# A graph layer on one core: other row loads, third convolution weights, planner's clock and order of streams

## The chip, the core and the metric

The kernel runs on one core of a Trainium2 chip. Its engines run side by side, each with its own queue of instructions: TensorE (PE, with its weight loads shown as PEld) multiplies matrices, VectorE (DVE) and ScalarE (ACT) work on tiles, GpSimd (POOL) does small operations and issues transfers, SyncE (SP) issues transfers. An engine works its queue in order; where an instruction needs a result of another engine or of a transfer, it waits for a semaphore, and all that is behind it in the queue waits too. The metric is the device time of one execution in microseconds (us); the median of several executions counts. Everything is computed in 32-bit floats.

## The reference, cut to what matters

There are 32 graphs of 512 nodes with 256 features (`x`), and a 0/1 matrix of 512 x 512 for each (`adj`). With `h = relu(layernorm(x))`, the output is `x` plus one graph layer of `h`:

```python
h1 = relu(bn1(conv1d(hT, conv1_w)))            # width 1, over the nodes
x_conv = relu(bn2(conv1d(h1, conv2_w, 8)) + hT)  # 17 taps, padding 8
s = h @ w_se.T + b_se                          # 3 numbers for a node
A = exp(-|s_n - s_m|^2) * adj
x_nmp = A @ relu(h @ w_msg.T + b_msg)
gi = concat(x_conv, x_nmp) @ w_ih.T + b_ih     # 512 -> 768
gh = h @ w_hh.T + b_hh                         # 256 -> 768
r, z = sigmoid(gi_r + gh_r), sigmoid(gi_z + gh_z)
out = x + (1 - z) * tanh(gi_n + r * gh_n) + z * h
```

## The kernel before

**Five streams.** The work is written as five generators (`streams`, from line 1778 on): *rows* makes the input of the long convolution (the width-1 convolution of each graph's turned features, `conv1`, line 528); *begins* turns the normalized features of later graphs, channels on partitions (`begin`, line 1230); *graphs* makes messages, the 512 x 512 kernel matrix, its masking and the gathering (`graph`, line 1282); *conv* is the convolution of 17 taps (`convolution`, line 980); *gates* computes the gates and the output (`gates`, line 1324), with seven products for a block of four times two for all graphs but the first and the last.

**The convolution.** The features of all graphs are cut into units of 18 nodes, and these into seven groups (`STARTS`). The 17 taps are not multiplied one by one: 25 products (numbered `m`, 25 to a group) of transformed inputs (`X2`, made on DVE by `operands`) with transformed weights are summed into the result (`summed`). A product has two weight matrices `w[0]`, `w[1]` of 128 x 2 x 256 and three input phases. In the first group four block products are formed for each `m`. In the later six groups three do: the third uses the sum `w[2] = w[0] + w[1]`, its result is copied to a second bank by ACT (`ps_c`), and the two others use differences of the inputs (`xd`, function `ends`). One product of the 25 (`LONE`, number 6) needs `w[1]` alone.

**Where weights come from.** In the first group `weights_first` (line 723) makes the 25 pairs on DVE and ACT, and `store_w` (line 720) stores each to a DRAM tile `WD[n]`, which has room for three, from POOL's queue. From the second group on `weights_again` (line 765) allocates tiles in a ring of six (`RING`, name `w`) and loads them on SP's queue. In the second group only `w[0]` and `w[1]` are loaded; `third_weight` (line 788) adds them on DVE into the third tile and stores that, from POOL, into `WD[n][:, 2]`. From the third group on all three are loaded. `third_weight` is called from the convolution for the product at hand and the next one, and from the background work (`background`, line 1700).

**Rows and their tiles.** The turned features of a graph are in DRAM (`HD[b]`, written by POOL). `load_row` (line 335) loads them on SP's queue into a tile named `hT`, of which there are two, for a convolution group that needs the graph; `begin` uses the same ring of two tiles for turning new graphs. In `all_rows` (line 1747) the next row's load is put off with `later` until about the time at which the planner's clock has a tile free.

**What sets the order.** All instructions are written in an order worked out while the program is built. A planner keeps a clock for each engine (`now` is that of PE): every operation is given a modelled duration and starts after the modelled ends of what it needs (`after`, line 126; `note`, line 139; `region`, line 102, gives the part of a tile that is touched). Transfers are modelled in `Engine.dma_start` (line 205) with an issue time, a flow rate and eight lanes in flight. A generator yields the time from which it can go on, or a condition. The loop at the end (line 1844 on) takes, among the streams that can go on now (`able`), the one whose own progress clock is least, except at those numbered choices where the table `OTHERS` names the second or third in that order instead. After each step `fill` (line 1722) writes what was put off (`later`), evacuates finished convolution results and, while DVE is free within 1.5 us of the clock, writes background work: norms, inputs and weights of the convolution, its sums, the third weights. The clock only orders instructions; on the chip each engine runs as its semaphores let it.

Of the kernel before, what the change touches and what calls it, by code (L numbers as in the profile page):

```python
# [10 lines left out]
ALU = mybir.AluOpType  # L11
PSUM = bass.MemoryType.PSUM
# [38 lines left out]
def kernel(  # L51
# [50 lines left out]
    def region(a):  # L102
        step = a.ap[0][0]
        size = 1 + sum((c - 1) * s for s, c in a.ap[1:])
        if a.tensor.name in ON_DRAM or step == 0:
            return 0, 1, a.offset, a.offset + size + step * (a.ap[0][1] - 1)
        p, f = divmod(a.offset, step)
        return p, p + a.ap[0][1], f, f + size
# [40 lines left out]
    class Pool:  # L149
        def __init__(self, pool, bufs, on_dram=False):  # L150
            self.pool, self.bufs, self.on_dram, self.rings = pool, bufs, on_dram, {}
            self.made, self.born = [], 0.0

        def tile(self, shape, dtype, **more):
            t = self.pool.tile(shape, dtype, **more)
            self.made.append(t.tensor.name)
            BORN[t.tensor.name] = self.born
            if self.on_dram:
                ON_DRAM.add(t.tensor.name)
            elif "name" in more:  # L160
                ring = self.rings.setdefault(more["name"], [])
                n = more.get("bufs", self.bufs)
                if len(ring) >= n:
                    BORN[t.tensor.name] = released(ring[-n]) + HAND
                ring.append(t.tensor.name)
            return t
# [7 lines left out]

    ON_DRAM = set()

    def pool_of(where, name, bufs, **more):
        pool = where.enter_context(tc.tile_pool(name=name, bufs=bufs, **more))
        return Pool(pool, bufs, more.get("space") == bass.MemoryType.DRAM)

# [19 lines left out]
    class Engine:  # L200
# [4 lines left out]
        def dma_start(self, dst, src, **more):  # L205
            run = 4 * min(dst.ap[-1][1], src.ap[-1][1])
            name = "P" if self.name == "POOL" else "H"
            lanes = LANES.setdefault(name, [0.0] * 8)
            at = max(self.free, after("DMA", [dst], [src]), lanes[0])
            if name == "P":  # L210
                issue = 1.1 if run < 512 else 0.78 if run == 1024 else 0.55
            else:
                issue = 0.53 if run < 512 else 0.43 if run == 1024 else 0.37
            self.free = at + issue
            rate = 150e3 if run < 512 else 330e3
            flow = (self.free + 1.85, 4 * elements(dst) * dst.shape[0] / rate)
            FLOW.append(flow)
            FLOW.sort()
            del FLOW[:-96]
            end = 0.0  # L220
            for arrives, cost in FLOW:
                end = max(end, arrives) + cost
                if (arrives, cost) == flow:
                    break
            lanes.pop(0)
            lanes.append(end)
            note("DMA", [dst], [src], end)
            self.engine.dma_start(dst, src, **more)  # L228
            return end
# [80 lines left out]
    XS, HT, HB, HR, HR_AT, HG, XN, XR = {}, {}, {}, {}, {}, {}, {}, {}  # L310
    NORMS, NORM_AT = {}, {}
    HD = {b: dram.tile([P, ND, N], F32, name=f"hd{b}") for b in range(B)}
# [16 lines left out]
    def load(b, xs=None):  # L329
# [3 lines left out]
        NORM_AT[b] = done(XS[b])  # L333

    def load_row(b):
        if b not in HR:
            settle_stores()
            HR[b] = front.tile([P, ND, N], F32, name="hT", bufs=2)
            sp.dma_start(HR[b], HD[b])
            HR_AT[b] = done(HR[b])  # L340
# [379 lines left out]
    def store_w(dst, src):  # L720
        later(act.free + 0.3, lambda: pool.dma_start(dst, src))

    def weights_first():

# [9 lines left out]
        for j1 in ORDER:  # L734
# [12 lines left out]
            for j2 in ORDER:  # L747
# [7 lines left out]
                for k in range(2):  # L755
                    for i in range(ND):
                        act.activation(
                            w[k][:, i, :], gg[i][:, k, :], AF.Copy, scale=GSCALE[j1] * GSCALE[j2]
                        )
                    store_w(WD[len(WS)][:, k], w[k])  # L760
                WS.append(w)
                W_AT.append(act.free + LAG)
                yield 0.0

    def weights_again():


        for m in range(25, 25 * NG):
            W_BASE.append(taken)
            w = {}  # L770
            for k in (1,) if m % 25 == LONE else (2, 0, 1):
                yield
                w[k] = new_w()
                if k < 2 or m >= 50:
                    sp.dma_start(w[k], WD[m % 25][:, k])
            WS.append(w)
# [4 lines left out]
    def load_weights(done):  # L781

        while len(WS) >= 25 and taken < done + RING and next(again, 0) is None:
            pass

    thirds = set()

    def third_weight(m):
        if m in thirds or m % 25 == LONE:
            return  # L790
        thirds.add(m)
        w = WS[m]
        dve.tensor_tensor(w[2], w[0], w[1], op=ALU.add)
        later(dve.free + 0.4, lambda: pool.dma_start(WD[m % 25][:, 2], w[2]))
        W_AT[m] = dve.free + LAG

# [183 lines left out]
    def convolution():  # L980
# [28 lines left out]
        for g in range(NG):  # L1009
# [9 lines left out]
            for n in range(25):  # L1019
# [8 lines left out]
                yield lambda: len(X2) > m and len(WS) > m  # L1028
                if 25 <= m + 1 < 50 and W_AT[m + 1] <= now:
                    third_weight(m + 1)  # L1030
                for k in (m, m + 1):
# [4 lines left out]
                if exp_waits:  # L1036
                    yield lambda: not exp_waits
                    yield bank_at
                if 25 <= m < 50:
                    third_weight(m)  # L1040
                    yield W_AT[m]
                w, x2 = WS[m], X2[m]
# [187 lines left out]
    def begin(b):  # L1230
# [4 lines left out]
        if b >= TURNED:  # L1235
# [6 lines left out]
            for o in range(ND):  # L1242
                blocks(xb[:, o, :], XD_[b].rearrange("(k i) d -> i k d", i=32), o)
            yield max(done(xb), front.free("hT", 2))
            settle_stores()
            HT[b] = front.tile([P, ND, N], F32, name="hT", bufs=2)
# [13 lines left out]
        yield lambda: b not in NORMS  # L1260
        yield NORM_AT[b]
        turning = True
        for d in range(ND):
# [436 lines left out]
    def background():  # L1700
# [9 lines left out]
        if sum_some():  # L1710
            return True
        for m in range(max(25, at_product), min(len(WS), 50)):
            if m not in thirds and m % 25 != LONE and W_AT[m] <= now:
                third_weight(m)
                return True
        for _ in range(3):
# [4 lines left out]

    def fill():
        while LATER and LATER[0][0] <= now:
# [3 lines left out]
        for b in (gating, gating + 1):  # L1727
            if b in HB:
                load_conv(b)
                if dve.free < now + 1.5:  # L1730
                    residual(b)
                    data_sums(b)
        while dve.free < now + 1.5 and background():
            pass
# [12 lines left out]
    def all_rows():  # L1747
# [5 lines left out]
        for g in range(1, NG):  # L1753
            for b in batches(g):
                yield lambda: (
                    freed >= g - 1 and begun > b and not turning and at_product >= 25 * g - 4
                )
                if b == batches(g)[0]:
                    zeros(g)
                rows_wait = True  # L1760
                yield front.free("hT", 2) - 0.5
                load_row(b)
                if b + 1 in batches(g) and b + 1 < begun:
# [6 lines left out]
    def all_gates():  # L1770
# [19 lines left out]
    OTHERS = {  # L1790
# [15 lines left out]
    }  # L1806
# [37 lines left out]
    while streams:  # L1844
# [11 lines left out]
        choices += len(able) > 1  # L1856
        name = able[min(OTHERS.get(choices, 0), len(able) - 1)] if len(able) > 1 else able[0]
        waits = 0
# [11 lines left out]
        elif got is not None:  # L1870
            clock[name] += (now - began) / streams[name][1]
        fill()

# [48 lines left out]
```

## Time and profile before

| | |
|---|---|
| runs (us) | 1994.66, 1997.48, 1999.35; median 1997.48 |
| the profiled execution | 1992.31 us, span 1990.5 us |
| granted TensorE clock, mean | 0.997 of full speed |
| PE busy | 1959.9 us, 98% of the span, 9691 matmuls |
| DVE / ACT / POOL busy | 1470.5 (74%) / 873.6 (44%) / 483.1 us (24%) |
| transfers | 378.91 MB, 190 GB/s over the span |
| weights: loads on SP / stores on POOL | 414 / 74, 256 KB each |

The span runs from the first to the last instruction of the profiled execution; its own time has a little more around it. Busy times of PE count modelled ends of pipelined matmuls, so "busy" is not yet full speed. A line like `PE ps_g L259 <- DMA hT<-hd: 3.2, 7, 1.0` in the view of waits reads: matmuls of line 259 writing `ps_g` waited for the transfer from `hd` to `hT`, 3.2 us in all, in 7 times, 1.0 us at longest. The lines 241, 259 and 228 are those of helpers through which all operations, matmuls and transfers go, so tiles tell them apart: `ps_c` is the convolution's bank, `ps_g` that of rows, messages and gathers, `ps_acc` that of the gates, `w` and `wd` the convolution's weights on chip and in DRAM, `hd` and `hT` the turned features in DRAM and on chip.

### The profile page before, as it was taken

How to read it: one execution, taken by the hardware profiler on the slowest of the kernel's cores; microseconds unless marked ns; L12 is line 12 of the kernel's file. 1: busy time of each engine (PE TensorE's matmuls, PEld its weight loads, DVE VectorE, ACT ScalarE, POOL GpSimd, SP SyncE). 2: the span in 40 equal slices, each digit the busy share in tenths (PEclk: the TensorE clock that was granted, in tenths of full speed). 3: DMA queues.
4: the chain of work that ended last, by engine and by line, in shares of the span. 5: the costliest groups of instructions: out<-in, count | busy, mean ns of one | idle time of the engine just before them, and what ended most of it. 6: DMA issues, size and time to landing. Idle time of an engine off the chain costs nothing. (4 is left out here: it accounts for less than half of the span.)

```text
span 1990.5 us, 28285 instructions
## 1 busy us (share of the span) xinstructions
PE 1959.9 (98%) x9691; PEld 1441.3 (72%) x9691; DVE 1470.5 (74%) x2559; ACT 873.6 (44%) x1755; POOL 483.1 (24%) x627
## 2 busy tenths in 40 slices
PE   8999999999999999999999999999999999999998
PEld 4877767768676777776777776777776777776774
DVE  6789788969888587875877776868784877765443
ACT  6654653354534455334463335453334453324221
POOL 2222122223112132212232122222221221113232
PEclk9999999999999999999999999999999999999999
DMA  7546878879898789879797888699976877576564
GB/s 272 178 172 216 276 233 206 222 191 240 224 231 215 183 199 207 205 186 224 161 240 172 209 179 230 172 235 202 207 164 179 183 181 157 154 153 125 94 101 35
DMA packets 578176, 378.91 MB, mean 190 GB/s; under 512 B 457664, under 2 KB 475488, under 8 KB 576896
## 3 DMA queue, kind: packets, MB, share of 16 engines
q1 hardware_dynamic: 419760, 279.15, 50.8%
q0 software_dynamic: 157184, 97.81, 26.8%
q8 instruction: 77, 1.26, 0.3%
q14 instruction: 67, 0.55, 0.1%
q10 hardware_dynamic: 1088, 0.13, 0.0%
HBM read 278.94 MB, written 114.56 MB: 198 GB/s over the span
## 5 line engine op out<-in xcount | busy, mean ns | idle before, releaser
L228 POOL DMA_DIRECT2D out_dram<-o_sb x252 | 276.1, 1719 | 583.2 <-DVE o_sb L241 528.6
L259 PEld LDWEIGHTS ps_c<-xd,w 128*128 128x128 f32 x2304 | 285.4, 190 | 44.9 <-ACT ps_c L241 32.2
L259 PEld LDWEIGHTS ps_c<-x,w 128*128 128x128 f32 x2032 | 256.7, 191 | 50.0 <-issue 32.3
L259 PE MATMUL ps_c<-xd,w 128*128 128x135 f32 (+1 forms) x2304 | 290.6, 279 | 1.9 <-ACT ps_c L241 1.4
L259 PE MATMUL ps_c<-x,w 128*128 128x135 f32 (+2 forms) x2032 | 265.6, 279 | 2.9 <-ACT z L241 2.2
L259 PE MATMUL ps_g<-at,msg 128*128 128x512 f32 x512 | 226.4, 593 | 1.5 <-DVE at L241 1.5
L241 DVE TENSOR_TENSOR ps_acc<-ps_acc,r 128x256 f32<-128x256 f32 x120 | 51.5, 429 | 233.8 <-PE ps_acc L259 217.3
L259 PE MATMUL ps_acc<-hTb,whh 128*128 128x512 f32 (+2 forms) x532 | 211.4, 495 | 0.5 <-ACT r L241 0.5
L259 PE MATMUL ps_acc<-xnb,wih 128*128 128x512 f32 (+2 forms) x532 | 209.7, 495 | 2.1 <-DVE ps_acc L241 2.1
L259 PE MATMUL ps_acc<-xconv,wih 128*128 128x512 f32 (+2 forms) x532 | 210.4, 493 | 0.2 <-DVE ps_acc L241 0.2
L259 PEld LDWEIGHTS ps_g<-at,msg 128*128 128x128 f32 x512 | 96.0, 190 | 113.5 <-issue 106.0
L259 PE MATMUL ps_acc<-t,wsum 128*128 128x256 f32 x720 | 175.2, 379 | 0.0
L259 PEld LDWEIGHTS ps_acc<-t,wsum 128*128 128x128 f32 x720 | 134.9, 190 | 33.4 <-issue 16.8
L259 PEld LDWEIGHTS ps_acc<-xconv,wih 128*128 128x128 f32 x532 | 98.6, 190 | 50.4 <-issue 41.4
L259 PE MATMUL ps_g<-wmsg,hTg 128*128 128x259 f32 x496 | 125.5, 383 | 1.9 <-DVE msg L241 1.9
L259 PEld LDWEIGHTS ps_acc<-xnb,wih 128*128 128x128 f32 x532 | 95.7, 190 | 40.7 <-issue 28.1
L259 PE MATMUL ps_acc<-t,wih 128*128 128x256 f32 x480 | 123.2, 379 | 0.0
L259 PEld LDWEIGHTS ps_acc<-hTb,whh 128*128 128x128 f32 x532 | 93.9, 190 | 39.2 <-issue 30.4
L259 PE MATMUL ps_g<-hT,w 128*128 128x512 f32 (+8 forms) x296 | 119.1, 549 | 3.2 <-DMA hT<-hd 3.2
L241 DVE TENSOR_TENSOR x<-x 128x544 f32<-128x544 f32 (+2 forms) x175 | 120.5, 707 | 0.3
L241 ACT ACTIVATE h<-ps_g,bn_shift,bn_scale 128x252 f32<-128x252 f32 (+8 forms) x212 | 87.0, 485 | 56.1 <-PE ps_g L259 55.9
L241 ACT ACTIVATE ps_c<-ps_c 128x270 f32<-128x270 f32 (+1 forms) x144 | 55.9, 388 | 126.2 <-PE ps_c L259 126.1
(156 smaller groups left out, 3202.0 us busy)
## 6 DMA issues: line engine op xcount, KB each, us to landing
w<-wd SPq DMA_DIRECT2D x414, 256.0 KB, 3.9
m_sb<-in_adj_dram SPq DMA_DIRECT2D x384, 64.0 KB, 3.8
wd<-w POOLq DMA_DIRECT2D x74, 256.0 KB, 3.5
hT<-hd SPq DMA_DIRECT2D x33, 512.0 KB, 4.5
hd<-hT POOLq DMA_DIRECT2D x32, 512.0 KB, 6.0
hTb<-hd SPq DMA_DIRECT2D x32, 512.0 KB, 4.8
xnb<-nd SPq DMA_DIRECT2D x64, 256.0 KB, 3.2
out_dram<-o_sb POOLq DMA_DIRECT2D x252, 64.0 KB, 4.8
```

Source lines behind the costliest of these rows:

```text
L228: self.engine.dma_start(dst, src, **more)
L241: getattr(self.engine, op)(*tiles, **more)
L259: nc.tensor.matmul(ps, lhsT, rhs, **more)
```

## The change

Row loads: `row_free` says whether the tile that the next `hT` would take is not one of a row still in use or of a graph being turned (`HTS` lists what took the tiles, None for a graph being turned). `load_row` does nothing while it is false; `all_rows` and `begin` wait for it.

Third weights: `store_sum` stores `w[0]` to `WD[n][:, 2]` and, at the planned end of that, adds `w[1]` to it by an accumulating store, both from POOL's queue, in the first group. In the second group `w[2]` is loaded like the others; `third_weight` is gone.

Clock: transfers are taken to land 1.0 us later, those of POOL another 0.75 us; POOL's issue of small runs is taken as 0.66 us in place of 1.1; a PSUM tile counts as touched as a whole.

Order: a new table `OTHERS`. A pick of 4 or 5 takes the first or second stream and leaves out the background work of the `fill` after it.

```diff
+        if a.tensor.name in ON_PSUM:
+            return 0, P, 0, N
         if a.tensor.name in ON_DRAM or step == 0:
...
             if name == "P":
-                issue = 1.1 if run < 512 else 0.78 if run == 1024 else 0.55
+                issue = 0.66 if run < 512 else 0.78 if run == 1024 else 0.55
...
-            flow = (self.free + 1.85, 4 * elements(dst) * dst.shape[0] / rate)
+            flow = (self.free + (2.6 if name == "P" else 1.85), 4 * elements(dst) * dst.shape[0] / rate)
...
             lanes.append(end)
+            end += 1.0
             note("DMA", [dst], [src], end)
...
+    def row_free():
+        return len(HTS) < 2 or not (HTS[-2] in HR or HTS[-2] is None and turning)
+
+    def row_in(b):
+        load_row(b)
+        return b in HR
+
     def load_row(b):
-        if b not in HR:
+        if b not in HR and row_free():
+            HTS.append(b)
             settle_stores()
...
+    def store_sum(dst, a, b):
+
+        def first():
+            end = pool.dma_start(dst, a)
+            later(end, lambda: pool.dma_start(dst, b, accum_op=ALU.add))
+
+        later(act.free + 0.3, first)
...
                     store_w(WD[len(WS)][:, k], w[k])
+                if len(WS) != LONE:
+                    store_sum(WD[len(WS)][:, 2], *w)
                 WS.append(w)
...
                 w[k] = new_w()
-                if k < 2 or m >= 50:
-                    sp.dma_start(w[k], WD[m % 25][:, k])
+                sp.dma_start(w[k], WD[m % 25][:, k])
...
-    thirds = set()
-
-    def third_weight(m):
-        if m in thirds or m % 25 == LONE:
-            return
-        thirds.add(m)
-        w = WS[m]
-        dve.tensor_tensor(w[2], w[0], w[1], op=ALU.add)
-        later(dve.free + 0.4, lambda: pool.dma_start(WD[m % 25][:, 2], w[2]))
-        W_AT[m] = dve.free + LAG
...
                 yield lambda: len(X2) > m and len(WS) > m
-                if 25 <= m + 1 < 50 and W_AT[m + 1] <= now:
-                    third_weight(m + 1)
...
-                if 25 <= m < 50:
-                    third_weight(m)
-                    yield W_AT[m]
...
             yield max(done(xb), front.free("hT", 2))
+            yield row_free
+            HTS.append(None)
             settle_stores()
...
         yield NORM_AT[b]
+        yield row_free
+        HTS.append(None)
         turning = True
...
-        for m in range(max(25, at_product), min(len(WS), 50)):
-            if m not in thirds and m % 25 != LONE and W_AT[m] <= now:
-                third_weight(m)
-                return True
...
-    def fill():
+    def fill(lean=False):
...
-        while dve.free < now + 1.5 and background():
+        while not lean and dve.free < now + 1.5 and background():
             pass
...
                     freed >= g - 1 and begun > b and not turning and at_product >= 25 * g - 4
+                    and (b in HR or row_free())
                 )
...
                 yield front.free("hT", 2) - 0.5
-                load_row(b)
+                yield lambda: row_in(b)
...
     OTHERS = {
-        8: 1, 11: 1, 41: 1, 43: 1, 57: 1, 70: 1, 73: 2, 84: 2, 95: 1, 102: 1, 104: 1, 110: 1,
...
+        1: 2, 8: 1, 16: 5, 35: 1, 39: 1, 52: 4, 55: 1, 62: 1, 86: 4, 87: 1, 98: 4, 108: 2, 118: 1,
...
-        name = able[min(OTHERS.get(choices, 0), len(able) - 1)] if len(able) > 1 else able[0]
+        pick = OTHERS.get(choices, 0) if len(able) > 1 else 0
+        name = able[min(pick % 4, len(able) - 1)]
...
-        fill()
+        fill(pick > 3)
```

More of the change, by code (lines that the diff above doesn't have):

```diff
@@ L149, with __init__ @@
     class Pool:
-        def __init__(self, pool, bufs, on_dram=False):
-            self.pool, self.bufs, self.on_dram, self.rings = pool, bufs, on_dram, {}
+        def __init__(self, pool, bufs, on_dram=False, on_psum=False):
+            self.pool, self.bufs, self.rings = pool, bufs, {}
+            self.on_dram, self.on_psum = on_dram, on_psum
             self.made, self.born = [], 0.0
@@ L157, in tile @@
             BORN[t.tensor.name] = self.born
+            if self.on_psum:
+                ON_PSUM.add(t.tensor.name)
             if self.on_dram:
@@ L173, in free @@
             return released(ring[-n]) + HAND if len(ring) >= n else 0.0
-    ON_DRAM = set()
+    ON_DRAM, ON_PSUM = set(), set()
     def pool_of(where, name, bufs, **more):
         pool = where.enter_context(tc.tile_pool(name=name, bufs=bufs, **more))
-        return Pool(pool, bufs, more.get("space") == bass.MemoryType.DRAM)
+        return Pool(pool, bufs, more.get("space") == bass.MemoryType.DRAM, more.get("space") == PSUM)
     const = pool_of(ctx, "const", 1)
@@ L310 @@
     XS, HT, HB, HR, HR_AT, HG, XN, XR = {}, {}, {}, {}, {}, {}, {}, {}
-    NORMS, NORM_AT = {}, {}
+    NORMS, NORM_AT, HTS = {}, {}, []
     HD = {b: dram.tile([P, ND, N], F32, name=f"hd{b}") for b in range(B)}
```

32 rows, old and new, of the table OTHERS are left out of this document.

## The prediction

> **What bounds the kernel now.** I read the page first, then the busy times by stage, then who made the tensor engine (PE) wait. The page says that PE is the bound almost everywhere:
>
> ```profile
> span 1990.5 us, 28285 instructions
> PE 1959.9 (98%) x9691; PEld 1441.3 (72%) x9691; DVE 1470.5 (74%) x2559; ACT 873.6 (44%) x1755; POOL 483.1 (24%) x627
> PE   8999999999999999999999999999999999999998
> ```
>
> PE is not busy for 1990.5 - 1959.9 = 30.6 us. The change adds and removes no needed matmul, so it can win only from these 30.6 us, and from matmuls that run slowly. Busy times by stretch of the span (PE, PEld, DVE, ACT, POOL, granted clock, DMA share, GB/s) show where they lie; the cuts are the start, the seven convolution groups as I read them off the trace, and the gates alone at the end:
>
> ```profile
> 0.00:50.00 50.00, 41.82 (x149) 24.41 (x150) 31.84 (x93) 30.39 (x66) 14.46 (x34) 0.93 0.74 271
> 100.00:250.00 150.00, 147.15 (x907) 114.14 (x908) 126.75 (x214) 80.93 (x188) 34.28 (x67) 1.00 0.68 220
> 250.00:512.00 262.00, 259.37 (x1342) 190.02 (x1341) 221.22 (x383) 121.39 (x246) 65.89 (x93) 1.00 0.84 222
> 512.00:760.00 248.00, 244.00 (x1211) 180.30 (x1210) 193.42 (x331) 113.31 (x230) 55.28 (x73) 0.99 0.87 209
> 1010.00:1260.00 250.00, 249.99 (x1211) 184.16 (x1211) 182.80 (x327) 107.68 (x221) 60.51 (x73) 1.00 0.84 199
> 1804.00:1990.00 186.00, 177.41 (x628) 117.20 (x626) 78.75 (x135) 57.02 (x87) 59.03 (x60) 1.00 0.57 91
> ```
>
> The start lacks 50.00 - 41.82 = 8.2 us and the end 186.00 - 177.41 = 8.6 us. At the start PE waits for the first data and norms; at the end the gates are the only stream left, so no order of streams exists there to change. What lies between, 30.6 - 8.2 - 8.6 = 13.8 us, is what an order can win. The stretch 1010 to 1260 shows that this can be nothing at all (249.99 of 250.00). The waits of PE from 50 to 1804 us (total, times, longest) name the causes:
>
> ```profile
> PE ps_g L259 <- DMA hT<-hd: 3.2, 7, 1.0
> PE ps_c L259 <- ACT z L241: 2.9, 3, 2.0
> PE ps_g L259 <- DVE msg L241: 1.9, 1, 1.9
> PE ps_g L259 <- DVE at L241: 1.5, 3, 0.8
> PE ps_c L259 <- ACT ps_c L241: 1.4, 3, 0.5
> PE ps_g L265 <- ACT hT L241: 0.7, 1, 0.7
> PE ps_c L259 <- ACT w L241: 0.6, 1, 0.6
> PE ps_c L259 <- DVE veps L241: 0.4, 1, 0.4
> PE ps_acc L259 <- DVE ps_acc L241: 0.2, 1, 0.2
> ```
>
> They sum to 12.8 us. No single wait owns them: each is a place where the written order sent PE to something that came later on the chip than the planner's clock thought. The longest also cost clock (same columns as the stretches above):
>
> ```profile
> 600.00:603.00 3.00, 0.96 (x3) 0.18 (x2) 2.78 (x4) 2.58 (x6) 0.40 (x2) 0.97 0.63 192
> 603.00:607.00 4.00, 4.00 (x18) 3.68 (x19) 4.00 (x8) 0.43 (x2) 0.58 (x1) 0.60 0.59 186
> ```
>
> After the 2.0 us stall near 600 us, 4.00 us ran at 0.60 of the clock: 4.00 x 0.40 = 1.6 us more. Within reach of the order: 12.8 + 1.6 = 14.4 us.
>
> **The change part by part.**
>
> *Third weights.* Removed: 24 adds on DVE, 24 stores of their result on POOL in the second group. Added: in the first group, after each of 24 weight pairs, one plain store and one accumulating store into the third slice, both on POOL (48 issues); in the second group, 24 loads of 256 KB on SP. The add, and what waited for it:
>
> ```profile
> L241 DVE TENSOR_TENSOR w<-w 128x512 f32<-128x512 f32 x24 | 16.3, 681 | 1.2 <-DMA w<-wd 1.2
> PEld ps_c L259 <- DVE w L241: 1.8, 3, 0.8
> PEld ps_c L259 <- DMA w<-wd: 3.0, 4, 0.8
> ```
>
> DVE gets back 24 x 0.681 = 16.3 us, but it is not the bound: in 250 to 512 us it is busy 221.22 of 262.00. Only the weight loads of PE waited for the add (1.8 us in 3 times), and they overlap matmuls; the matmul waits above have no row for it. The gain lies between 0 and 1.8 us; I take 0.5, since the prefetching weight load had most of it to spare. Against it stands that the third weight now comes by a load, and weight loads waiting for landings cost PEld 3.0 us over the kernel, so the loss is at most as large again. I set the two together at 0.
>
> The stores use the POOL queue and the DMA engines of the first group. POOL row, landing times and the ACT writes of the weights up to 236 us, then the DMA load of 42 to 232 us:
>
> ```profile
> L228 POOL DMA_DIRECT2D wd<-w x50: 539/540/602, 42.6 to 211.8; - x50
> DMA to landing us min/median/max: 2.3/3.4/13.6
> L241 ACT ACTIVATE w<-gg x60: 399/408/438, 41.6 to 211.0; 128x256 f32<-128x256 f32 x60
> 42.00:232.00 190.00, 27.13 (x50) 1.00 0.62 210
> q0 software_dynamic: 6240, 20.98, 28.7%
> ```
>
> POOL: 48 x 0.540 = 25.9 us more in 190 us, where in 100 to 250 us it is busy 34.28 of 150.00. The accumulating store waits for the plain one to land, at the head of POOL's queue if it is issued early; the planner issues it only when its own clock says landed. Behind it on POOL wait stores of normalized rows and messages, and the small powers that finish the norms (ACT's norms wait for those, and the turned rows for ACT). With the median of 3.4 us hardly any wait remains; with the longest of 13.6 us a single one costs about 10. Tiles: 25 pairs in 211.8 - 42.6 = 169.2 us are one in 7.0 us; the ring of six holds three pairs, so a pair's buffers are wanted again after 21 us. It is now held for about three issues and two landings, 1.6 + 3.4 + 3.4 = 8.4 us, far less. I take 0 for both.
>
> DMA engines: an accumulating store of 256 KB is not in the trace. Below it lies a plain one: queue q0, POOL's, moved 20.98 MB in 6240 packets, and took 28.7% of 190 us, 54.5 us of all engines, so 0.26 MB takes 0.68 us. Above it lies the accumulating store of the output, in the last stretch (1870 to 1980 us):
>
> ```profile
> q0 software_dynamic: 16896, 2.10, 39.2%
> out_dram<-o_sb POOLq DMA_DIRECT2D x32, 64.0 KB, 3.9
> ```
>
> 39.2% of 110 us over 32 stores is 1.35 us for 64 KB; at the same rate per byte 256 KB takes 5.4 us. These stores consist of 16896 / 32 = 528 small packets each, against 6240 packets for ten times the bytes of all 32 above, so the price is mostly per packet and a store of weights lies nearer the plain one: I take 1.5 us. The added load is 24 x (0.68 + 1.5) = 52 us in 190, share 0.62 to 0.90; between the ends 33 us (0.79) and 146 us (1.39). From 50 to 250 us PE waited for a DMA once:
>
> ```profile
> PE ps_g L259 <- DMA hT<-hd: 0.2, 1, 0.2
> ```
>
> The loads are issued ahead; at 0.90 they land slightly later, and I take a loss of 0.5 us. The second group moves as much as before (24 loads for 24 stores).
>
> The row says POOL issues never starved here (longest 602 ns). The Trainium skill (SBUF — State Buffer, Who interferes with whom) has a rule against this part: while DVE runs a two-port mode, GpSimd cannot write the descriptors of a transfer issued from POOL, which so stalls. By it 48 more such issues beside a DVE that is busy 126.75 of 150 us would each be late; in this trace's first group the issue time does not show that, so the sum keeps 0.540 us.
>
> *Row loads wait for a free tile.* A load of a row is no longer put in SP's queue before the last reader of its tile is. SP's waits, and the worst row load:
>
> ```profile
> SPq L228 <- PE ps_c L259: 449.8, 182, 10.2
> SPq L228 <- PE ps_g L259: 129.3, 38, 16.8
> 1494.17 0.94 SPq L228 DMA_DIRECT2D hT<-hd  x2
> 1500.09 0.84 PE L259 MATMUL ps_g<-hT,w 128*128 128x341 f32 x2 [1.01 <-DMA hT<-hd]
> ```
>
> A load that heads SP's queue unready holds weights, masks and graph rows behind it: 129.3 us of SP waits end with a matmul that read rows, masks or messages. The gain is at most the 3.2 us that PE waited for rows; the loss, if the guard starts a row later and nothing covers it, one landing: the load issued at 1494.2 reached PE at 1500.1, 5.9 us, against 1.0 us of stall there. The same guard holds back the turning of new rows, whose stores and graph loads queue behind it on POOL and SP. I take a gain of 1 us. The 24 new loads of the third weights wait in SP's queue for a weight tile too, as those of the later groups do (449.8 us, 182 times); from 1010 to 1260 us this did PE no harm, so I take 0.
>
> *The clock and the order.* Landings 1.0 us later (POOL's 0.75 more), shorter POOL issues for small runs and whole PSUM banks cost no instruction; they change what the planner believes ready, and with the new table and its picks that leave DVE's background work for later, every choice of stream. Bounds: all 14.4 us gone, or as much again added. I take half of the 14.4 less the row's 1 us already counted, (14.4 - 1.0) / 2 = 6.7 us, as stalls are single events that better landings should partly avoid, while a new order makes some of its own. For the start I take 0 of its 8.2 us.
>
> There the skill reads otherwise: TensorE: Matmul & The Clock Gate (What's actually happening) has the clock throttled after an idle window of about 3.4 us. The trace disagrees, since a 2.0 us stall among slack work was enough; by the page the 1.6 us would not be there and the sum would be 0.8 us smaller.
>
> **Sum.** 0 - 0.5 + 1.0 + 6.7 = 7.2 us faster. The profiled execution took 1992.31 us, of which the span is 1990.5; it would take 1985.1. The median of the runs, 1997.48 us, lies 5.2 us above it, and I carry that over: 1997.48 - 7.2 = 1990.3 us.
>
> **The rivals.**
>
> *The stalls only move.* The old order had its late places, the new has as many others: 1997.5 us. For it: the causes above are nine kinds on three engines and DMA, so a table of choices does not remove a cause. Against it: rows and bank hand-overs, 3.2 + 1.4 us, are just what the new clock times differently.
>
> *Nearly all goes.* The middle group shows 250 us without a stall; were every group like it, 14.4 us go, and of the start's 8.2 us perhaps 4: 1997.5 - 18.4 = 1979 us. Against it: the same order made that group and the others.
>
> *Transfers bound the first group* (slower). Free DMA time there is 0.38 x 190 = 72 us; first stores take 24 x 0.68 = 16, so sums decide from (72 - 16) / 24 = 2.3 us each. At 3.0 us, the middle between 0.68 and 5.4, they overflow by 24 x 0.7 = 17 us; masks, rows and messages land late, and PE stands still for most of it: 1997.5 + 15 = 2012 us. For it: 1.35 us for a quarter of the bytes. Against it: the small packets.
>
> *The guard does nothing*: rows load when they did, 1 us of the sum is missing, 1991.3 us; this lies inside the forecast's range.
>
> **How the numbers follow.** Forecast 0.55, with a range of its own of 1984 to 1996 (a gain of 1.5 to 13.5 us); stalls only move 0.20; nearly all goes 0.11; transfers bound the first group 0.14. The range of 1980 to 2004 us leaves out about half of the third case and most of the last, under 0.2. A measurement of this kernel can tell about 0.2%, 4 us, from no change. Faster, below 1993.5: 0.44 of the forecast's 0.55 and 0.11, so 0.55. Same: the other 0.10, and 0.14 of the moving stalls, 0.24. Slower: 0.14, 0.06 of the moving stalls and 0.01 of the forecast, 0.21.
>
> **What would show it.** Right: PE busy within 3 us of 1959.9 less the slow clock's 1.6, idle between 50 and 1804 us near 6; no adds on weights on DVE; a share near 0.90 in the first group with landings of weight stores under 6 us; fewer waits of PE for rows; no stretch at 0.60 of the clock after the start. Wrong: new PE waits of over 2 us in the second or third group; the first group ending later than before; POOL waiting for its own stores with the norms late behind; idle time at the start that moves by over 3 us either way, which I priced at nothing.

## The result and the profile after

The changed kernel took 1976.45 us (median of 4 executions, 1974.95 to 1977.93), the kernel before 1996.07 us beside it (4 executions, 1993.70 to 1999.35): a ratio of 0.990 with a 95% interval of 0.988 to 0.992. Measured again with 6 and 12 executions (run e9 below) it was 1976.96 against 1992.42 us, 0.992 (0.991 to 0.994). The kernel before moves by some us from one series of runs to the next: beside the experiments its medians are 1989.51 to 1992.42 us. The changed kernel's two medians lie 0.5 us apart. So the gain is 15 to 20 us, and nearer 15 by the later series. I had forecast 7.2, with a range of 1980 to 2004: the direction was right, the size was not.

The two traces lie closer than the medians. That of before is an execution of 1992.31 us, 3.8 us under its median of four; that of the changed kernel is one of 1977.93 us, 1.5 us over its own. They explain 1990.5 - 1976.1 = 14.4 us of span. The page of the changed kernel:

```profile
span 1976.1 us, 28304 instructions
PE 1955.7 (99%) x9691; PEld 1442.1 (73%) x9691; DVE 1458.9 (74%) x2535; ACT 872.4 (44%) x1755; POOL 499.6 (25%) x651
```

The matmuls are the same 9691. Idle time of PE fell from 30.6 to 1976.1 - 1955.7 = 20.4 us, and busy time by 1959.9 - 1955.7 = 4.2 us, though the work is the same. Busy times by stretch (PE, PEld, DVE, ACT, POOL, granted clock, DMA share, GB/s) show where:

```profile
0.00:50.00 50.00, 43.32 (x165) 26.51 (x166) 30.34 (x97) 31.55 (x67) 20.06 (x43) 0.97 0.89 318
100.00:250.00 150.00, 148.85 (x902) 114.48 (x901) 125.35 (x201) 78.84 (x181) 55.08 (x95) 0.99 0.93 278
250.00:512.00 262.00, 260.32 (x1343) 190.75 (x1342) 210.38 (x372) 122.16 (x249) 55.59 (x73) 1.00 0.87 222
512.00:760.00 248.00, 248.00 (x1188) 180.82 (x1187) 186.67 (x323) 113.87 (x225) 58.85 (x78) 1.00 0.87 205
760.00:1010.00 250.00, 250.00 (x1292) 191.20 (x1291) 204.42 (x349) 109.94 (x228) 56.27 (x69) 1.00 0.88 214
1790.00:1975.00 185.00, 177.83 (x624) 116.47 (x622) 78.96 (x135) 57.13 (x87) 58.96 (x60) 1.00 0.57 91
```

From 512 to 1010 us PE has no idle time at all, where before it lacked 4.0 us in the first half of that alone; the gain is largest there, in the third group. The start still lacks 6.7 us (8.2 before). The waits of PE from 50 us to the end of the last group at 1790 us (total, times, longest):

```profile
PE ps_acc L265 <- ACT right L247: 1.4, 1, 1.4
PE ps_g L265 <- DMA hT<-hd: 1.2, 2, 1.1
PE ps_c L265 <- ACT ps_c L247: 1.0, 2, 0.6
PE ps_c L265 <- ACT z L247: 0.7, 1, 0.7
PE ps_c L265 <- DVE x L247: 0.5, 1, 0.5
PE ps_g L265 <- ACT h L247: 0.3, 1, 0.3
```

They sum to 5.1 us against 12.8 before. The two longest of before, 2.0 us for `z` near 600 us and 1.9 us for a message, are gone, and row loads stop PE twice instead of seven times.

The fall of the busy time doesn't come from the clock: its mean is 0.997 in both traces, and each has two slow stretches between the first 20 us and the end (near 33 and 603 us; near 57 and 214 us). Part of it lies in how busy time adds up. Two lines of the trace of before, one of the groups of matmuls (265.6 us is their busy time together, 279 ns the mean of one) and one of five matmuls in a row:

```profile
L259 PE MATMUL ps_c<-x,w 128*128 128x135 f32 (+2 forms) x2032 | 265.6, 279 | 2.9 <-ACT z L241 2.2 <-ACT w L241 0.6
595.84 0.74 PE L259 MATMUL ps_c<-x,w 128*128 128x136 f32 x5
```

In a row each begins before the one ahead of it ends, so it adds only (740 - 279) / 4 = 115 ns. One that stands alone ahead of a gap adds all of its 279 ns, 164 more. The whole views of waits count 40 waits of PE before and 24 after. By an estimate that takes this for matmuls of all kinds, 16 x 0.164 = 2.6 of the 4.2 us are thus a price of waits beyond their length. Where the rest lies is open.

### The profile page after: what moved, and what is told of

Same layout as the page of the kernel before. It is cut to its first block, busy times and chain, and to the rows that moved or that the text cites. A ratio compares the mean times of both kernels' runs of the same rounds, so it can differ in the third digit from the quotient of the medians.

```text
span 1976.1 us, 28304 instructions
## 1 busy us (share of the span) xinstructions
PE 1955.7 (99%) x9691; PEld 1442.1 (73%) x9691; DVE 1458.9 (74%) x2535; ACT 872.4 (44%) x1755; POOL 499.6 (25%) x651
## 4 chain that ended last, share of the span: by engine, by line
PE 93%; DVE 3%; DMA 1%; ACT 1%; issue 1%; POOL 0%; SPq 0%; DVEq 0%; ACTq 0%; POOLq 0%
PE ps_acc L265 44%; PE ps_c L265 26%; PE ps_g L265 21%; PE ps_g L271 2%; DVE t L247 1%; DVE o_sb L247 1%; DMA hT<-hd 1%; DMA x_sb<-in_x_dram 1%; DVE x L247 0%; DVE st L247 0%; DVE g L247 0%; DVE ps_acc L247 0%; ACT h L247 0%; ACT at L247 0%; DVE z L247 0%
## 5 line engine op out<-in xcount | busy, mean ns | idle before, releaser
L247 DVE TENSOR_TENSOR msg<-ps_g,bmsg 128x259 f32<-128x259 f32 x128 | 53.1, 420 | 81.4 <-PE ps_g L265 81.3
```

The lines of the kernel that those rows point to most:

```text
L247: getattr(self.engine, op)(*tiles, **more)
```

## The experiments

Order and parts of the change are hard to take apart here: any change of the planner's clock or of a pick changes the order of everything behind it. So the first kernels below keep the written order of the matmuls exactly and alter only what is sent to DVE, POOL and SP; the later ones change the order on purpose.

### The third weights, with the order kept

**e1.** The changed kernel with the adds on DVE again, each written just ahead of the product of `m - 1` or, where the planner did not yet take the weights as landed, ahead of its own. `ghost` has the planner count a transfer that is not sent.

```diff
-            end = pool.dma_start(dst, a)
-            later(end, lambda: pool.dma_start(dst, b, accum_op=ALU.add))
+            end = pool.dma_start(dst, a, ghost=True)
+            later(end, lambda: pool.dma_start(dst, b, ghost=True))
...
-                sp.dma_start(w[k], WD[m % 25][:, k])
+                sp.dma_start(w[k], WD[m % 25][:, k], ghost=k == 2 and m < 50)
...
+                if 25 <= m + 1 < 50 and len(WS) > m + 1 and W_AT[m + 1] <= now:
+                    third_weight(m + 1)
...
+                if 25 <= m < 50:
+                    third_weight(m)
                 w, x2 = WS[m], X2[m]
```

> The changed kernel with its order of matmuls kept exactly; only the third weights go back: in the second group DVE adds the two loaded weights (24 adds, not counted by the planner's clock) and POOL stores the sums, and the two stores of the sum in the first group and the 24 loads in the second are left out. Order theory (the new order took the stalls away, the third weights are worth about nothing): within 3 us of the changed kernel's 1976.5, so under 1980. Transfer theory (the 16.3 us that DVE got back let PE go on): 8 to 16 us slower, 1984 to 1992, with new PE waits for DVE between 240 and 510 us.

Measured: 2034.22 us, ratio 1.021 (1.019 to 1.023) to the kernel before, some 57 us slower than the changed kernel. Neither theory had that. PE waits of this run:

```profile
PE ps_c L266 <- DVE w L817: 36.7, 17, 4.0
```

The adds take 0.68 us each as before; but written at the product they can stand behind 1.5 us or more of background work in DVE's queue, and the planner, which does not know of them, sends PE into the product at once. That is a test of bad timing, not of the adds' price. The next two write the adds earlier:

**e5 and e10.** The same kernel twice; each add is now written in `fill`, as soon as the loads of its two weights count as landed.

```diff
+        for m in range(max(25, at_product), min(len(WS), 50)):
+            if W_AT[m] - 1.0 <= now:
+                third_weight(m)
         if EVAC:
```

> As the run before with the adds on DVE and the changed kernel's order of matmuls, but each add is written as soon as the planner takes its two loads as landed, not at the product that needs it. If the earlier run's 36.7 us of PE waits came from adds written late behind DVE's background work: 1977 to 1990, PE waits for these adds under 8 us. Transfer theory (DVE has no room for the adds in this order): still above 2010.

> The changed kernel itself, beside the kernel before and the next run on one chip. Both theories: 0.990 to 0.993 of the kernel before.

> The changed kernel's order of matmuls with the third weights added early on DVE, again, beside the changed kernel on one chip. If the third weights by transfers are worth something by themselves: 3 to 6 us slower than the changed kernel, all of it between 250 and 520 us. If they are worth nothing, as I forecast: within 2 us of it.

Measured: e5 1981.60 us, ratio 0.995 (0.993 to 0.996). Then beside the changed kernel on one chip with 6 executions each: changed (e9) 1976.96 (1976.03 to 1978.57), early adds (e10) 1980.68 (1979.87 to 1982.79). The third weights by transfers are thus worth 3.7 us in this order, and the other 1992.42 - 1980.68 = 11.7 us of the gain measured there remain with the adds on DVE: they belong to the order and to what makes it (guard, clock and table). The place, 250 to 512 us, first e9 and then e10 (columns as above):

```profile
250.00:512.00 262.00, 261.43 (x1356) 193.26 (x1353) 211.28 (x375) 124.09 (x252) 56.07 (x73) 1.00 0.89 224
```

```profile
250.00:512.00 262.00, 257.79 (x1328) 187.93 (x1327) 219.00 (x386) 120.15 (x245) 65.62 (x92) 1.00 0.86 221
```

PE lacks 0.6 us with the transfers and 4.2 us with the adds: 3.6 us, about the whole difference. The other trace of each kernel lacks 1.7 (the changed kernel's first) and 4.2 us (e5), so 2.5 to 3.6 us is the surer figure for the place. Hardly any of it is a wait for an add itself. PE waits of e10 in 236 to 520 us, the first five of eight lines, where e9 has the wait of the third alone:

```profile
PE ps_c L266 <- ACT n L248: 0.9, 1, 0.9
PE ps_acc L266 <- DVE wsum L248: 0.9, 1, 0.9
PE ps_c L266 <- ACT ps_c L248: 0.6, 1, 0.6
PE ps_g L266 <- DMA hT<-hd: 0.5, 1, 0.5
PE ps_c L266 <- DVE w L817: 0.5, 1, 0.5
```

The adds are the last line. That the others come from DVE, and with it ACT, running later behind 24 more operations fits (DVE is busy 219.00 against 211.28 us there), but no run shows it.

**e2.** The changed kernel without the accumulating store.

```diff
-            later(end, lambda: pool.dma_start(dst, b, accum_op=ALU.add))
+            later(end, lambda: pool.dma_start(dst, b, ghost=True, accum_op=ALU.add))
```

> The changed kernel in its order; the accumulating store of the third weights is left out (the third weights are then wrong: the first weight alone). Order theory and my price of 1.5 us of all DMA engines a store, hidden: within 2 us of 1976.5. If transfers press on the first group: 2 to 6 us faster, with the DMA share of 42 to 232 us well lower and fewer PE waits before 250 us.

Measured: 1976.99 us, ratio 0.992 (0.991 to 0.994): the same as the changed kernel. The 24 accumulating stores cost no time that the runs can tell (the 24 plain ones are still sent); what they cost in transfers shows in 42 to 232 us, the stores' row by stretch (POOL, granted clock, DMA share, GB/s) and POOL's transfers, first of the changed kernel, then of e2:

```profile
42.00:232.00 190.00, 58.40 (x92) 0.98 0.87 252
q0 software_dynamic: 11052, 31.58, 58.8%
```

```profile
42.00:232.00 190.00, 36.67 (x68) 0.99 0.66 224
q0 software_dynamic: 7595, 25.28, 35.7%
```

24 accumulating stores take (58.8 - 35.7)% of 190 us = 43.9 us of all DMA engines, 1.83 us each, in (11052 - 7595) / 24 = 144 packets.

**e6.** The other way round: the kernel before in its own order, with the sums by transfers, which its planner does not count.

```diff
+            nc.gpsimd.dma_start(dst, a)
+            later(now + 6.0, lambda: nc.gpsimd.dma_start(dst, b, accum_op=ALU.add))
...
                 if k < 2 or m >= 50:
                     sp.dma_start(w[k], WD[m % 25][:, k])
+                else:
+                    nc.sync.dma_start(w[k], WD[m % 25][:, k])
...
-        dve.tensor_tensor(w[2], w[0], w[1], op=ALU.add)
+        dve.tensor_tensor(w[2], w[0], w[1], op=ALU.add, ghost=True)
```

> The kernel before with its order of matmuls kept exactly; only the third weights change: the 24 adds on DVE and the stores of their results are left out, the first group stores the sums by transfers and the second group loads them. Order theory: within 3 us of the kernel before (1992 to 1996). Transfer theory: 5 to 15 us faster.

Measured: 2003.00 us against 1991.11, ratio 1.005 (1.004 to 1.007), slower by 12 us in the medians and 10 in the means (one of its nine executions took 1994.84). Both theories missed. The loss lies mostly in the first group (columns as above; the kernel before was busy for 147.15 us there):

```profile
100.00:250.00 150.00, 138.67 (x840) 105.84 (x840) 117.55 (x197) 72.12 (x173) 57.60 (x98) 0.98 0.92 273
```

PE waits from 50 to 250 us, where the kernel before had 0.2 us of this kind, and waits of POOL up to 236 us:

```profile
PE ps_g L261 <- DMA hT<-hd: 6.7, 2, 4.4
```

```profile
POOL wd L729 <- DMA wd<-w: 43.5, 16, 5.6
```

The accumulating stores wait at the head of POOL's queue for the plain ones to land. Behind them stands a store of normalized rows (`xd<-x_sb`), and the transfers that read it head SP's queue ahead of a row load. One case in order of time:

```profile
194.63 0.90 POOL L729 DMA_DIRECT2D wd<-w  x1 [1.52 <-DMA wd<-w]
197.97 0.85 POOL L729 DMA_DIRECT2D wd<-w  x1 [2.44 <-DMA wd<-w]
198.53 1.10 POOL L229 DMA_DIRECT2D xd<-x_sb  x1
205.06 4.49 SPq L229 DMA_DIRECT2D x_sb<-xd  x8
209.65 0.43 SPq L229 DMA_DIRECT2D hT<-hd  x1
213.85 3.67 PE L261 MATMUL ps_g<-hT,w 128*128 128x512 f32 x8 [2.31 <-DMA hT<-hd]
```

In the kernel before the same store was issued at 192.11 us and the same row load at 200.73. The changed kernel has waits of the same kind on POOL:

```profile
POOL wd L234 <- DMA wd<-w: 53.0, 15, 10.0
```

There PE does not suffer: its row waits up to 250 us are none, and e2 without the accumulating stores took the same time. Its planner counts the stores and can send PE elsewhere; that this is the reason is argued, as the two kernels differ in their whole order.

### The table and the clock

**e3, e4, e7.** The changed kernel with the old table; with an empty one; the kernel before with an empty one.

```diff
-    OTHERS = {
...
+    OTHERS = {}
```

> The changed kernel with the table of choices of the kernel before. Table theory (the table is what removes stalls, and it fits only the clock it was made with): 1988 to 2002, about as slow as with no table. Clock theory (a clock that lands transfers later and counts banks whole writes a better order by itself): under 1984.

> The changed kernel with an empty table: every choice goes to the stream that is furthest behind. Table theory: 1988 to 2002. Clock theory: under 1984.

> The kernel before with an empty table. Table theory: 2015 to 2035, as slow as the changed kernel without its table (2025.8), so that both tables are worth 25 to 50 us and the new one about 15 more. Clock theory (the new clock writes a better order by itself): at least 8 us slower than 2025.8.

Measured: 2021.54 us (ratio 1.015, 1.013 to 1.016), 2025.77 (1.017, 1.015 to 1.020) and 2032.38 (1.020, 1.017 to 1.022). For e3 and e4 both theories were too fast, by some 20 us or more. An old table fits the new planner hardly better than none (4 us). Without tables both kernels are some 30 to 40 us slower than the kernel before as it stands: the new table is worth 2025.77 - 1976.96 = 49 us to its kernel, the old one 2032.38 - 1991.11 = 41 us to its own. The new table is thus worth some 8 us more than the old one, where I had expected 15.

**e11 and e12.** How local is a table's gain? e11 drops the 74 picks behind choice 1398; e12 drops one pick of the 194, choice 35.

```diff
-        1: 2, 8: 1, 16: 5, 35: 1, 39: 1, 52: 4, 55: 1, 62: 1, 86: 4, 87: 1, 98: 4, 108: 2, 118: 1,
+        1: 2, 8: 1, 16: 5, 39: 1, 52: 4, 55: 1, 62: 1, 86: 4, 87: 1, 98: 4, 108: 2, 118: 1,
```

> The changed kernel with the picks of its table up to choice 1398 kept and the 74 later ones dropped; the order of matmuls is the same up to about 1030 us. Table theory: the same as the changed kernel up to there, and 10 to 25 us of new waits behind it, 1985 to 2000 in all. Clock theory: under 1982.

> The changed kernel with one pick of its 194 left out (choice 35, near the start); all choices behind it fall otherwise. Table theory (the picks fit only the very order they were made for): 2005 to 2030, as slow as without a table. If each pick is a gain by itself: within 3 us of the changed kernel.

Measured: e11 1983.22 us (ratio 0.995, 0.994 to 0.997), 6.3 us slower than the changed kernel beside it; e12 2040.96 us (1.024, 1.022 to 1.026), 64 us slower. The late picks are worth less than I expected, and one early pick less costs more than no table at all. The waits of e12 are large and of all kinds, these the first four:

```profile
PE ps_c L265 <- ACT z L247: 9.4, 6, 3.4
PE ps_acc L265 <- DVE ps_acc L247: 6.1, 10, 1.8
PE ps_g L265 <- DMA hT<-hd: 5.4, 3, 3.3
PE ps_c L265 <- ACT right L247: 5.1, 1, 5.1
```

So this pick is not a gain by itself: the table selects one whole order, and here the picks behind choice 35 were worth nothing once that choice fell otherwise. Other single picks were not tried.

**e8, e13 to e18.** Does the new clock write better orders by itself? Four untuned orders (empty table; picks 20, 110, 150; picks 110, 204, 256; picks 1, 150, 189, 310), each under the new and the old clock, with the guard and the third weights of the change in all.

```diff
-        if a.tensor.name in ON_PSUM:
-            return 0, P, 0, N
...
-                issue = 0.66 if run < 512 else 0.78 if run == 1024 else 0.55
+                issue = 1.1 if run < 512 else 0.78 if run == 1024 else 0.55
...
-            flow = (self.free + (2.6 if name == "P" else 1.85), 4 * elements(dst) * dst.shape[0] / rate)
+            flow = (self.free + 1.85, 4 * elements(dst) * dst.shape[0] / rate)
...
-            end += 1.0
```

> The changed kernel with an empty table and the clock of the kernel before (landings, POOL's issue time, parts of banks); row guard and third weights by transfers stay. Clock theory: at least 8 us slower than 2025.8 with the new clock. Table theory: within 8 us of it, either way.

> The changed kernel with an empty table but for picks 20, 110 and 150 (1 each), so another untuned order, under the new clock. If the new clock by itself writes better orders: faster than its partner with the old clock by 10 us or more, as with the empty table (2025.8 against 2055.3). If that pair was chance, as one pick can move 60 us: either sign.

> The partner with the old clock: 2030 to 2070 if the clock matters, and more PE waits for row loads than the new clock's; otherwise anywhere from 2010 to 2060.

> A third untuned order (picks 110: 1, 204: 2, 256: 2 alone) under the new clock. Clock theory: 10 us or more faster than its partner; chance: either sign.

> Its partner with the old clock: 2030 to 2070 if the clock matters; otherwise anywhere from 2010 to 2060.

> A fourth untuned order (picks 1: 2, 150: 1, 189: 2, 310: 2 alone) under the new clock. Clock theory: 10 us or more faster than its partner; chance: either sign.

> Its partner with the old clock: 2030 to 2070 if the clock matters; otherwise anywhere from 2010 to 2060.

| picks | new clock (us) | old clock (us) | difference |
|---|---|---|---|
| none (e4, e8) | 2025.77 | 2055.34 | 29.6 |
| 20, 110, 150 (e13, e14) | 2010.48 | 2035.93 | 25.5 |
| 110, 204, 256 (e15, e16) | 2018.08 | 2029.47 | 11.4 |
| 1, 150, 189, 310 (e17, e18) | 2031.22 | 2044.64 | 13.4 |

All four go the same way, by 20 us on the mean, though one order differs from the next by as much. The kernel before without a table (e7) makes another pair with e8: both have the old clock, and with the guard and the third weights by transfers e8 is 2055.34 - 2032.38 = 23 us slower. So without an order made for them these two parts need not help at all; one pair of untuned orders gives no price. PE waits of three kinds under the new clock and then the old one, empty table (the two traces lie 41 us apart, more than the medians; that of e8 is its slowest execution):

```profile
PE ps_c L265 <- ACT ps_c L247: 6.4, 6, 4.1
PE ps_acc L265 <- DVE ps_acc L247: 3.0, 8, 1.0
PE ps_g L265 <- DMA hT<-hd: 2.0, 2, 1.4
```

```profile
PE ps_g L262 <- DMA hT<-hd: 12.9, 6, 5.5
PE ps_c L262 <- ACT ps_c L244: 9.0, 10, 2.2
PE ps_acc L262 <- DVE ps_acc L244: 7.6, 12, 2.5
```

Waits for row loads (12.9 to 2.0 us) and for banks handed between engines fall. Over all four pairs the wait for rows falls in three and that for the banks of the convolution (`ps_c`) in all, while that for the gates' banks rises in three, so the waits fall where transfers land and at the convolution's banks; which part of the clock does it was not tried apart.

No experiment gave a kernel faster than the changed one.

## Why the prediction was wrong, point by point

- **What bounds.** Right in the main: the same matmuls, PE the bound, and the gain is stalls that went. They went from the third group above all, as the stretches show. "It can win only from these 30.6 us, and from matmuls that run slowly" was too narrow: 4.2 of the 14.4 us between the traces are busy time at an unchanged mean clock.
- **Third weights, set at 0.** Wrong by 3.7 us. The step that failed is "the matmul waits above have no row for it": PE hardly waits for the adds themselves (0.5 us in e10), yet with them it lacks up to 3.6 us more, which the waits put down to other tiles. The freed 16.3 us of DVE were worth about a quarter of themselves. e1 shows the same adds costing 57 us when they are written late, so the price is one of timing.
- **Transfers of the first group.** The size was near: 1.83 us of all DMA engines a store where I took 1.5, a share of 0.87 where I expected 0.90, and no loss of time (e2) where I took 0.5. That it was near is partly luck, as the price is not mostly per packet: the store has 144 packets, the one of 64 KB has 528 and takes 1.35 us. "I take 0 for both" was wrong for POOL's waits: POOL waited 53.0 us for its own stores. That it cost nothing here is probably the work of the planner: in e6, whose planner does not count them, waits of this kind came with a loss of 10 to 12 us. My rival of a slower first group had the wrong price but a real place: POOL's queue rather than the DMA engines' time.
- **Row loads, 1 us.** PE waited 2.0 us less for them in the middle (3.2 to 1.2). How much of this is the guard's and how much the clock's can't be told: a kernel without the guard has another order from the start, and that was not tried. So the rival "the guard does nothing" stays open.
- **Clock and order, half of what remains.** This is the term that was mis-sized, together with what the sum had at nothing beside it. The sum's 6.7 + 1.0 us stood for 6.9 us of waits and 0.8 us of slow clock. The middle's waits fell by 7.7 of their 12.8 us, so the share of waits that go was near. But half was a guess between ends, with no row that said how good the old clock was, so that it was near is luck. The slow clock gave nothing: the slow stretches near 33 and 603 us went, and others came near 57 and 214. What the sum had at nothing is the rest: PE's busy time fell by 4.2 us, of which by estimate 2.6 are what waits cost beyond their length, and idle time fell by 1.5 us at the start and 0.8 at the end (from 1804 and 1790 us on). Together these are the 14.4 us between the traces, against 7.2.
- **The base.** The forecast of 1990.3 us lay 13.9 us too high: 7.2 by the gain, the other 6.7 by the base. I carried 5.2 us from the profiled execution of before to its median over to the changed kernel, whose profiled execution is 1.5 us over its median. These are spreads of executions: in the later series the median of before lay near that profiled execution's 1992.31 us or below it (1989.51 to 1992.42).
- **The causes apart.** Of 15.5 us, 3.7 are the third weights (e9, e10). The other 11.7 are the order, and guard, clock and table were not taken apart in it. The pairs of untuned orders say that the new clock alone is worth 11 to 30 us there, which need not be so in a tuned order.
- **The rivals.** "Nearly all goes" (1979 us) came nearest, with a chance of 0.11, yet not as it was told: the middle's waits went by three fifths, not wholly. The reach of 14.4 us that bounded it left out the end and most of the busy time. "The stalls only move" fell.
- **What would show it.** PE busy (1955.7, expected within 3 us of 1958.3), idle time of PE between the start and the end (5.4 us by stretch, expected near 6), no add on DVE, the share and the landings (median 4.7 us, longest 11.3) came as told. Of the signs of being wrong one came, POOL waiting for its own stores, and without a loss. "No stretch at 0.60 of the clock after the start" did not come, as the last section shows.

## What to carry to other kernels

When work moves between queues, look first at when it is queued and whether the thing that writes the order knows of it: the same 24 adds cost 4 or 57 us by when they were written; the accumulating stores cost nothing in the order made with them, and all 48 stores with their loads cost 10 to 12 us in one that did not count them. An engine at 84% that PE does not visibly wait for can still be worth relieving: here 3.7 us where I took 0. A tuned table of choices belongs to the exact program it was tuned on: price a change without a table for both programs, on several orders, and expect little from an old table.

## What the runs showed of the hardware that I had not expected

The granted clock can fall while PE is hardly idle. In the clock records of all 20 traces it is 1.00 or 0.50, and at 0.50 it stays for 3.41 us or a multiple of that (but where the span ends). Here are stretches of 3.41 us with their successors (columns as above): in the kernel before, a stretch and the slow one behind it; in the changed kernel the same; then, for the changed kernel, the first of its two with the matmuls of five rows alone (tile `right`):

```profile
599.39:602.81 3.42, 1.40 (x7) 0.57 (x5) 3.19 (x6) 2.40 (x6) 0.81 (x2) 1.00 0.69 222
602.81:606.22 3.41, 3.40 (x12) 3.11 (x13) 3.41 (x6) 0.62 (x2) 0.77 (x1) 0.50 0.51 161
210.28:213.69 3.41, 3.12 (x21) 1.81 (x16) 0.20 (x1) 3.18 (x8) 2.31 (x4) 1.00 0.96 166
213.69:217.11 3.42, 3.42 (x11) 2.20 (x11) 0.45 (x1) 0.01 (x1) 0.00 (x0) 0.50 1.04 374
210.28:213.69 3.41, 1.67 (x8) 0.29 (x2) 0.00 (x0) 0.00 (x0) 0.00 (x0) 1.00 0.96 166
```

In the kernel before PE was idle for 2.0 us of the stretch. In the changed kernel it was idle for 0.29 us, but matmuls of five rows (of 128) took 1.67 us, which leaves about 1.5 us for matmuls of all 128 rows; in the kernel before it was 1.40 us. e9 is the same program with the same five-row matmuls. If the stretches are counted on in steps of 3.41 us from its own slow one at 54.39 us, they cut those matmuls in two:

```profile
207.98:211.40 3.42, 1.13 (x6) 0.31 (x6) 0.00 (x0) 0.00 (x0) 0.00 (x0) 1.00 0.77 141
211.40:214.81 3.41, 1.12 (x2) 0.29 (x2) 0.00 (x0) 0.00 (x0) 0.00 (x0) 1.00 1.08 314
```

PE was busy for 3.20 and 3.34 us of them, so 2.1 and 2.2 us of full rows were left, and the clock stayed at 1.00. Counted in this way over the 20 traces, behind their first 20 us, all 100 stretches at full clock with under 1.4 us of 128-row matmuls were followed by the slow clock, and none of some 11,000 with over 1.8 us; in between it went either way. So in this case the clock goes by the work of full rows within a fixed stretch, and the same order meets a slow stretch or not by where the stretches fall. The Trainium skill (TensorE: Matmul & The Clock Gate, What's actually happening) has the clock fall after an idle window of about 3.4 us that runs freely; the length and the free run agree, but PE was busy for 3.12 of the 3.41 us here. So the 2.0 us stall that I set against the page fits it too, if the window need not be idle throughout.

An accumulating store of 256 KB takes 1.83 us of the DMA engines with 144 packets, and one of 64 KB took 1.35 us with 528; a plain store of 256 KB took 0.68 us. So neither the bytes nor the packets alone set the price.
